# Another program order for the ranking stage of layer 1 in a four-layer graph network

## The chip, the cores and the metric

One core of a Trainium2 chip runs the whole program in one launch. The metric is the device time in microseconds (us); the figure of a kernel is the median of its runs. Five engines work from queues of their own, each in the order of the program: TensorE (PE, with its weight loads shown as PEld), VectorE (DVE), ScalarE (ACT), GpSimd (POOL) and SyncE (SP, which issues most transfers).

## The reference

Four residual layers work on 2708 nodes with 128 features and one dense 2708 x 2708 matrix `adj`. Layer 1, in which the change lies, is a graph attention:

```python
h = jnp.maximum(_layernorm(x), 0.0)
XW = jnp.matmul(h, W)
s_col = jnp.matmul(XW, a[0, :f])
s_row = jnp.matmul(XW, a[0, f:])
Z1 = leaky_relu(s_row[:, None] + s_col[None, :], negative_slope=0.01)
den = jnp.exp(Z1)
num = jnp.matmul(A, den)
att = jnp.where(num != 0, den / jnp.where(num != 0, num, 1.0), 0.0)
x = x + jnp.matmul(A, jnp.matmul(att, XW))
```

`den[i, j]` depends on the two terms `s_row[i]` and `s_col[j]` alone and has a kink where their sum is zero. So the kernel does not multiply `A` by the whole of `den`: it sorts the nodes by `s_row`, takes running sums of the sorted rows of `A` (the "knots"), and for each column picks the two knots around its own kink.

## The kernel before, in words

The nodes lie in T = 22 tiles of 128 (the last has 20), in six groups of four tiles (`GROUPS`, the last has two). The 2708 columns are cut into six pieces of 512 (`KBS`, the last has 148). The stage of the change ranks the nodes by their row term and begins at line 1519 with one loop over the 22 tiles. PE, DVE, ACT and some POOL instructions are pinned (`pe`, `dve`, `act`, `pin`): each engine executes them in the order in which the Python code emits them, so moving a call in the loop moves its instructions in the queue of each engine that it uses.

For each tile t the loop calls:

- `mask(t)` (DVE): a bf16 row of ones where a later node's row term is not above that of the tile's node. Three buffers (`flags`, bufs=3) hold the masks of tiles 1 to 21, so `mask(t)` waits until PE and ACT are done with the mask of tile t - 3. `mask0` has a buffer of its own. Masks get shorter with t, since only columns from the tile on are compared.
- `summed(t)` (ACT): the mask's sum along the row, into `later`; its written copy (`lists`) is a by-product. Tiles 2, 19 and 20 (`SUMMED_HERE`) are summed by DVE while the mask is made.
- `counts(t)` (PE): ones times the mask, added up over the tiles in the two PSUM tiles `cnt`.

Every four tiles a group's counts are complete. `count_row(b)` (ACT) copies them out as a row, `count_turn(b)` (PE) turns that row into a column of `c_ps`, and `ranked(b)` (DVE) takes from it `later` and a constant, which gives the rank of each node. `listed(t0, t1)` (DVE, seven operations) turns ranks into a tile and a place and builds one-hot lists; `joined(t0, t1)` (PE, two matmuls for each tile) adds these lists into the PSUM tile `sp`. When all 22 tiles are joined, `sp` holds for every sorted place the number of its node; DVE copies that into `src_u`, and POOL starts the gathers `mov<-in_adj_dram` with it (`fetch`).

Between these run three others:

- `totals(n)` (PE): the next n block sums. One of them is 16 matmuls over a tile of `adj` with the weights `w_a` (the first eight, FRONT = 8) or `w_n` (the others), into two PSUM tiles `tot`, which shows in the profile as `acc<-chunk,w_a` and the like (`res`, `chunkY`, `chunkU` are other buffers of the same). The argument `TOTALS` says after which tile how many are done: four block sums (0 to 3) run ahead of the loop, 17 in it, one after it. When block sum 7 is done, ACT copies its two halves out with a factor (`act.mul`, output `tots`), and the PSUM tiles are taken anew by block sum 8. SP loads the matrix tiles (line 1233); each load waits for a buffer that an earlier block sum releases.
- `column_terms(g)` (PE): the column terms of group g, eight matmuls for four tiles, into `c_ps`.
- `column_max()` and `node_terms()` (DVE, PE, POOL, ACT): the greatest column term, and factors made of it that are read behind the stage.

`split_terms()` (POOL) is not touched. Where a helper records an operation, the profile names line 84 for it, so groups are told apart by their tiles: `mask`, `lists` (ACT: the mask sums), `row`, `tots`, `rank`, `later`, `tile_of`, `in_tile`, `in_place`, `in_tile_v`, `ps<-mask,ones_b` (counts), `acc<-ident,row` (count turns), `acc<-wga,h1T` (column terms), `acc<-in_tile_v,in_place` and `acc<-lists` (joins).

Of the kernel before, what the change touches and what calls it, by code (L numbers as in the profile page):

```python
# [8 lines left out]
F32 = mybir.dt.float32  # L9
# [8 lines left out]
P = 128  # L18
# [6 lines left out]
def kernel(  # L25
# [21 lines left out]
    T = -(-N // P)  # L47
# [14 lines left out]
    keep = ctx.enter_context(tc.tile_pool(name="keep", bufs=1))  # L62
# [23 lines left out]
    pe, dve, act = Ordered(nc.tensor), Ordered(nc.vector), Ordered(nc.scalar)  # L86
# [683 lines left out]
    FRONT = 8  # L770
# [298 lines left out]
    def column_terms(g):  # L1069
        for t in range(*GROUPS[g]):  # L1070
            pin(
                nc.tensor.matmul(
                    c_ps[0][: width(t), CC + t : CC + t + 1], hT[:, cols(t)], wga[:, 0:1], start=True, stop=True
                )
            )
# [105 lines left out]
    hi, rmax, part = vec("hi", 1), vec("rmax", 1), vec("part", 1)  # L1181
# [19 lines left out]
    tot = [acc(1), acc(2)]  # L1201
    QUARTER = N // 4
    SPLIT = QUARTER // 2
# [33 lines left out]
    so_far, tots = [0], []  # L1237

    def totals(n):
        for x_ in range(so_far[0], so_far[0] + n):  # L1240
            t = todo[x_]
            w = width(t)
            c = early.pop(t, None) or total_chunk(t)
            if x_ == FRONT:
                tot[:] = [acc(1), acc(2)]
            ws_ = w_a if x_ < FRONT else w_n
            for half in range(2):
                for g in range(4):
                    k0 = QUARTER * g + SPLIT * half
                    n_ = (SPLIT, QUARTER - SPLIT)[half]  # L1250
                    pe.matmul(
                        tot[half][32 * g : 32 * g + 32, :n_],
                        ws_[:w, t : t + 1].to_broadcast([w, 32]),
                        c[:w, k0 : k0 + n_],
                        start=(x_ in (0, FRONT)),
                        stop=(x_ in (FRONT - 1, T - 1)),
                    )
            if x_ == FRONT - 1:
                tots.append(keep.tile([P, QUARTER], F32, name="tots", tag="own"))
                for half in range(2):  # L1260
                    x0 = tots[0][:, SPLIT * half : (SPLIT, QUARTER)[half]]
                    act.mul(x0, tot[half][:, : x0.shape[1]], part)
        so_far[0] += n

    totals(1)
    terms_turned(E3 - 1)
# [98 lines left out]
    def summed(t):  # L1365
        w, a = width(t), t * P
        if t not in SUMMED_HERE:
            act.activation(
                seen[:w, a:], masks[t][:w, a:], AF.Copy, accum_out=later[:w, t : t + 1]
            )  # L1370

    def counts(t):
        w, a = width(t), t * P
        mk = masks.pop(t)
        for b, (k0, n) in enumerate(KBS):
            c0, c1 = max(a, k0), k0 + n
            if c0 >= c1:
                continue
            g = 32 * (b % 4)
            pe.matmul(  # L1380
                cnt[b // 4][g : g + 32, c0 - k0 : c1 - k0],
                ones_b[:w, :32],
                mk[:w, c0:c1],
                start=(t == 0),
                stop=(a + w == k0 + n),
            )
# [9 lines left out]
    def count_turn(b):  # L1396
        row = count_rows.pop(b)
        for t in range(*GROUPS[b]):
            o = (t - GROUPS[b][0]) * P
            pe.transpose(  # L1400
                c_ps[0][: width(t), CC + 32 + t : CC + 33 + t], row[:, o : o + width(t)], ident[:1, :1]
            )

    def ranked(b):
        t0, t1 = GROUPS[b]
        for t in range(t0, t1):
            if t in SUMMED_HERE:
                dve.tensor_tensor(
                    later[:, t : t + 1], later[:, t : t + 1], own_later[t], ALU.add
                )  # L1410
        dve.tensor_tensor(
            later[:, t0:t1], later[:, t0:t1], behind[:, t0:t1], ALU.subtract
        )
        for c0, c1, w in ((t0, min(t1, T - 1), P), (max(t0, T - 1), t1, TAIL)):
            if c0 < c1:
                dve.tensor_tensor(
                    rank[:w, c0:c1], c_ps[0][:w, CC + 32 + c0 : CC + 32 + c1], later[:w, c0:c1], ALU.subtract
                )
# [7 lines left out]
    def in_spare(first):  # L1426
        box(
            first,
            8,
            (  # L1430
                spare.tile([P, 8, T], BF16, name="in_tile"),
                spare.tile([P, 8, P + 3], BF16, name="in_place"),
                spare.tile([P, 5, 8, T], BF16, name="in_tile_v"),
            ),
        )
# [11 lines left out]
    def listed(t0, t1):  # L1447

        n = t1 - t0
        (ta, pl, tv), i = boxes[t0]  # L1450
        r_, a_, m_ = rank[:, t0:t1], tile_of[:, t0:t1], at_of[:, t0:t1]
        dve.tensor_scalar(a_, r_, -(PER + 1) / 2.0, 1.0 / PER, op0=ALU.add, op1=ALU.mult)
        dve.tensor_scalar(a_, a_, 1.5 * BIG, None, op0=ALU.add)
        dve.tensor_scalar(a_, a_, -1.5 * BIG, None, op0=ALU.add)
        dve.scalar_tensor_tensor(m_, a_, -float(PER), r_, op0=ALU.mult, op1=ALU.add)
        dve.tensor_tensor(
            ta[:, i : i + n, :],
            at_tile[:, None, :].to_broadcast([P, n, T]),
            a_[:, :, None].to_broadcast([P, n, T]),
            ALU.is_equal,  # L1460
        )
        dve.tensor_tensor(
            pl[:, i : i + n, :],
            at_place[:, None, :].to_broadcast([P, n, P + 3]),
            m_[:, :, None].to_broadcast([P, n, P + 3]),
            ALU.is_equal,
        )
        dve.tensor_tensor(
            tv[:, :, i : i + n, :],
            ta[:, None, i : i + n, :].to_broadcast([P, 5, n, T]),  # L1470
            vals[:, :, t0:t1, None].to_broadcast([P, 5, n, T]),
            ALU.mult,
        )

    def joined(t0, t1):
        for t in range(t0, t1):
            (_, pl, tv), i = boxes.pop(t)
            w = width(t)
            pe.matmul(
                sp[:3, :LIST].rearrange("p (v t) -> p v t", t=T)[:, 2:, 1:],  # L1480
                pl[:w, i, DUP],
                tv[:w, 2:, i, : T - 1],
                start=False,
                stop=False,
            )
            pe.matmul(
                sp[:, :LIST], pl[:w, i, :P], tv[:w, :, i, :], start=False, stop=(t == T - 1)
            )
# [6 lines left out]
    def column_max():  # L1495
        dve.tensor_copy(c_nat[:, : T - 1], c_ps[0][:, CC : CC + T - 1])
        dve.tensor_copy(c_nat[:TAIL, T - 1 :], c_ps[0][:TAIL, CC + T - 1 : CC + T])
        dve.tensor_reduce(c_hi, c_nat, AX.X, ALU.max)
        pe.matmul(
            c_ps[0][:, 256:384], c_hi.to_broadcast([P, P]), ident, start=True, stop=True  # L1500
        )

    def node_terms():
        dve.tensor_reduce(cmax, c_ps[0][:, 256:384], AX.X, ALU.max)
        dve.tensor_scalar(cmx, cmax, rmax, -1.0, op0=ALU.add, op1=ALU.mult)
        pin(nc.gpsimd.tensor_scalar(c_n, c_nat, rmax, None, op0=ALU.add))
        pin(nc.gpsimd.tensor_scalar(hb, c_n, 0.0, -0.495, op0=ALU.max, op1=ALU.mult))
        act.activation(s_n, c_n, AF.Exp, scale=0.99)
        act.activation(sig, hb, AF.Exp)
# [6 lines left out]
        pin(nc.gpsimd.tensor_tensor(parts_of_r[:, 1, :], parts_of_r[:, 0, :], vals[:, 3, :], ALU.subtract))  # L1516
        pin(nc.gpsimd.tensor_copy(vals[:, 4, :], parts_of_r[:, 1, :]))

    TOTALS = {2: 2, 10: 2, **{t: 1 for t in (0, 1, 4, 5, 6, 7, 8, 9, 12, 13, 14, 16, 18)}}
    for t in range(T):  # L1520
        mask(t)
        if t % 4 == 1 and 5 <= t < T - 1:
            ranked(t // 4 - 1)
        if t == 1:
            split_terms()
        if t == 5:
            column_max()
        if t == 6:
            node_terms()
        if t == 10:  # L1530
            in_spare(0)
            listed(0, 8)
        if t == 14:
            in_spare(8)
            listed(8, 12)
        summed(t)
        counts(t)
        if t % 4 == 3:
            count_row(t // 4)
        if t % 4 == 0 and t:  # L1540
            count_turn(t // 4 - 1)
        if t == 11:
            joined(0, 8)
        if t == 15:
            joined(8, 12)
        if t in (1, 2, 3, 4):
            column_terms(t + 1)
        totals(TOTALS.get(t, 0))
    listed(12, 16)
    in_lists(16, T - 16)  # L1550
    ranked(4)
    listed(16, 20)
# [1 line left out]
    count_turn(5)  # L1554
    ranked(5)
    listed(20, T)
    joined(12, T)


    sg = lay.tile([P, N], BF16, name="sg", tag="H")  # L1560
# [89 lines left out]
    for half in range(2):  # L1650
        x0 = tots[0][:, SPLIT * half : (SPLIT, QUARTER)[half]]
# [353 lines left out]
```

## Time and profile before

| | |
|---|---|
| median of 3 runs | 1107.77 us (1105.91 to 1108.09) |
| the profiled execution | 1104.28 us, span 1102.6 us |
| PE busy | 993.3 us (90% of the span), 3553 instructions |
| DVE busy | 582.5 us (53%), 1194 instructions |
| ACT busy | 401.0 us (36%), 629 instructions |
| POOL busy | 228.7 us (21%), 248 instructions |
| DMA | 282.72 MB, mean 256 GB/s |

The busy shares are means over very different stages. The loop over the 22 tiles lies between about 420 and 468 us of the span; the gathers of sorted rows and the writing of knots follow up to about 615 us, the attention up to about 776 us, and layers 2 and 3 fill the rest. The profile names the chain of work that ended last, gives each instruction's start and length by engine, what ended the idle time ahead of it, and the clock that TensorE was granted in any window (1.00 is the full clock). Times of matmuls overlap a little, because they are pipelined and their ends are modelled. All times in the text are from the start of the span.

### The profile page before, as it was taken

To read this page: it belongs to the slowest core of one execution; us is meant where nothing else is said; L and a number is where in the kernel's file an instruction comes from. 1 tells how busy PE (TensorE), PEld (TensorE's weight loads), DVE (VectorE), ACT (ScalarE), POOL (GpSimd) and SP (SyncE) were. 2 spreads that over 40 slices of the span, in tenths; PEclk is the share of its full clock that TensorE was granted. 3 is DMA by queue.
4 is the path that set the end of the run, shared out by engine and by line. 5 is a ranking of instruction groups with operands and counts; after the bars stand their busy time and mean duration, and the time that the engine had idled before them with its cause. 6 is when DMAs were issued, how large, how long until landed. Compare 5 with 4: busy or idle time off the path is not lost.

```text
span 1102.6 us, 10164 instructions
## 1 busy us (share of the span) xinstructions
PE 993.3 (90%) x3553; PEld 485.9 (44%) x3553; DVE 582.5 (53%) x1194; ACT 401.0 (36%) x629; POOL 228.7 (21%) x248
## 2 busy tenths in 40 slices
PE   6999999999999988899787277777999999999998
PEld 5444443444344455554333133333444455455444
DVE  5366368999852266757466489998210321032003
ACT  5100045444300067568765287786200210021000
POOL 2000000000199781023232145551000000000000
PEclk9999999999999998989999769999999999999999
DMA  9997220004389349399999899999999257716811
GB/s 271 342 321 250 66 74 9 0 1 174 132 351 408 113 141 421 131 351 425 420 417 402 292 425 431 428 433 388 398 345 391 88 208 275 264 60 211 303 42 51
DMA packets 48323, 282.72 MB, mean 256 GB/s; under 512 B 6478, under 2 KB 17834, under 8 KB 28660
## 3 DMA queue, kind: packets, MB, share of 16 engines
q1 hardware_dynamic: 38191, 189.13, 45.9%
q0 software_dynamic: 9840, 92.94, 20.9%
q8 instruction: 28, 0.46, 0.2%
q14 instruction: 24, 0.20, 0.0%
q10 hardware_dynamic: 240, 0.00, 0.0%
HBM read 250.06 MB, written 33.00 MB: 257 GB/s over the span
## 4 chain that ended last, share of the span: by engine, by line
PE 66%; DMA 20%; DVE 6%; ACT 3%; issue 3%; POOL 1%; SPq 0%; DVEq 0%; POOLq 0%; ACTq 0%
PE acc L404 34%; PE acc L84 15%; PE acc L806 10%; DMA pair<-table,pair_u 10%; DMA mov<-in_adj_dram,src_u 6%; PE ps L84 3%; DVE att L84 2%; DMA chunk<-in_adj_dram 2%; PE ps L384 1%; ACT att L84 1%; DMA held<-in_adj_dram 1%; PE acc L814 1%; DMA gath<-ydr,near_p 1%; DMA w<-in_L_gnn_W_dram 1%; ACT sg L1567 1%
## 5 line engine op out<-in xcount | busy, mean ns | idle before, releaser
L84 PE MATMUL acc<-att,xw 128*128 128x512 f32 (+2 forms) x264 | 110.6, 570 | 54.3 <-DVE att L84 54.2
L404 PE MATMUL acc<-chunk,h 128*128 128x512 f32 (+1 forms) x384 | 148.0, 542 | 0.0
L84 PE MATMUL acc<-mov,wt 128*128 128x512 f32 (+1 forms) x264 | 109.9, 562 | 19.4 <-DVE mov L84 19.2
L806 PE MATMUL acc<-zT 128*128 128x512 f32 (+2 forms) x264 | 112.3, 559 | 0.0
L404 PEld LDWEIGHTS acc<-chunk,h 128*128 128x128 f32 x384 | 68.8, 190 | 74.1 <-issue 74.1
L84 PEld LDWEIGHTS acc<-att,xw 128*128 128x128 f32 (+1 forms) x264 | 50.0, 197 | 114.8 <-issue 82.6
L942 POOL DMA_INDIRECT gath<-ydr,near_u x63 | 65.1, 1034 | 153.8 <-DMA ydr<-y 140.6
L404 PE MATMUL acc<-chunk,y 128*128 128x512 f32 x204 | 80.2, 553 | 3.9 <-DMA chunk<-in_adj_dram 3.0
L84 PEld LDWEIGHTS acc<-mov,wt 128*128 128x128 f32 x264 | 47.4, 192 | 81.6 <-DVE mov L84 48.0
L821 ACT COPY strip<-acc 128x512 f32<-128x512 f32 (+1 forms) x132 | 60.4, 560 | 59.2 <-issue 35.8
L1790 POOL DMA_INDIRECT pair<-table,pair_u x22 | 64.1, 2913 | 78.6 <-DVE att L84 52.7
L84 DVE SCALAR_TENSOR_TENSOR att<-pair,kap 128x2708 f32<-128x2708 f32 (+3 forms) x24 | 67.1, 2803 | 22.6 <-DMA pair<-table,pair_u 22.6
L84 DVE COPY mov<-knots 2x512 f32<-2x512 f32 x126 | 46.5, 394 | 53.1 <-DMA mov<-in_adj_dram,src_u 32.1
L404 PE MATMUL acc<-chunk,attended 128*128 128x512 f32 x192 | 73.1, 542 | 0.0
L84 ACT ACTIVATE att<-att,sca 128x2708 f32<-128x2708 f32 (+3 forms) x24 | 56.7, 2362 | 41.7 <-DVE att L84 29.0
L84 DVE SCALAR_TENSOR_TENSOR att<-row_all,inv_s,att 128x2708 f32<-128x2708 f32 (+3 forms) x24 | 67.1, 2798 | 3.8 <-ACT att L84 3.8
L823 DVE MAX8 top_v<-strip 128x8 f32<-128x2708 f32 (+1 forms) x22 | 64.7, 2965 | 7.3 <-ACT strip L821 7.3
L806 PEld LDWEIGHTS acc<-zT 128*128 128x128 f32 (+1 forms) x264 | 45.1, 185 | 51.3 <-issue 43.8
L404 PEld LDWEIGHTS acc<-chunk,y 128*128 128x128 f32 x204 | 37.3, 193 | 46.0 <-issue 44.7
L84 ACT ACTIVATE att<-att,hb 128x2708 f32<-128x2708 f32 (+3 forms) x24 | 56.7, 2364 | 0.8
L1567 ACT ACTIVATE sg<-row_all,c_nat 128x2708 bf16<-128x2708 f32 (+1 forms) x22 | 56.4, 2564 | 0.1
L84 ACT COPY knots<-acc 128x512 f32<-128x512 f32 x66 | 37.3, 594 | 42.4 <-PE acc L84 42.2
(379 smaller groups left out, 1277.4 us busy)
## 6 DMA issues: line engine op xcount, KB each, us to landing
chunk<-in_adj_dram SPq DMA_DIRECT2D x75, 1354.0 KB
table<-knots SPq DMA_DIRECT2D x19, 1354.0 KB
res<-in_adj_dram SPq DMA_DIRECT2D x9, 1354.0 KB
held<-in_adj_dram SPq DMA_DIRECT2D x11, 512.0 KB
held<-in_adj_dram SPq DMA_DIRECT2D x16, 256.0 KB
upper<-in_adj_dram SPq DMA_DIRECT2D x4, 842.0 KB
held<-in_adj_dram SPq DMA_DIRECT2D x3, 1024.0 KB
chunkY<-in_adj_dram SPq DMA_DIRECT2D x2, 1354.0 KB
```

Of the source, the lines that this page charges most:

```text
L84: return lambda *a, **k: pin(getattr(self.engine, name)(*a, **k))
L384: mm = nc.tensor.matmul(p[: width(t), t - t0, :], srcT[:, cols(t)], w, start=True, stop=True)
L404: nc.tensor.matmul(out[b][:, :n], y[r, tile_at(i), :], chunk(i)[r, k0 : k0 + n], start=(i == 0), stop=(i == T - 2),)
L806: mm = nc.tensor.matmul(zz[b][:w, :n], zT[:, cols(t)], zT[:, k0 : k0 + n], start=True, stop=False)
L814: nc.tensor.matmul(zz[b][:w, :n], ones_b[g : g + 3, :w], sq_rows[g : g + 3, k0 : k0 + n], start=False, stop=True,)
L821: copied = nc.scalar.copy(s[:w, k0 : k0 + n], zz[b][:w, :n])
L823: nc.vector.max(top_v[:w, t, :], s[:w, :])
L942: nc.gpsimd.indirect_dma_start(out=g[: idx.shape[0], :], out_offset=None, in_=ydr[:, :], in_offset=bass.IndirectOffsetOnAxis(ap=idx, axis=0),)
L1567: nc.scalar.activation(sg[:w, :], row_all[:w, :], AF.Sign, bias=c_nat[:w, t : t + 1], accum_out=signs[:w, t : t + 1],)
L1790: nc.gpsimd.indirect_dma_start(out=r[:w].rearrange("p a n -> p (a n)"), out_offset=None, in_=table[:, :], in_offset=bass.IndirectOffsetOnA ...
```

## The change

It changes only where the calls of this stage stand. The factor copies become a function of their own, `front_total`, called at tile 5 behind the mask sum of that tile instead of right behind block sum 7 (at tile 2). `TOTALS` spreads the same 17 block sums differently. Count turns come at tiles 5, 9, 13, 17 and 20 instead of 4, 8, 12, 16 and 20. The ranks of groups 0 and 1 are taken together at tile 10, those of groups 2 and 3 together at tile 18, instead of one group at each of tiles 5, 9, 13 and 17. The listings are 0 to 7 at tile 10, 8 to 15 at tile 18, then 16 to 19 and 20 to 21 behind the loop; before they were 0 to 7 at tile 10, 8 to 11 at tile 14, and 12 to 15, 16 to 19 and 20 to 21 behind the loop. The joins follow at tiles 12 and 19 and behind the loop. The column terms of groups 2 to 5 move from tiles 1 to 4 to tiles 3 to 6, the column maximum from tile 5 to 12 and the node terms from 6 to 13. The operations are the same, but for the two listings of four tiles that become one of eight, seven DVE instructions for fourteen (DVE has 6 instruction rows fewer, the other engines as many as before).

```diff
--- before.py
+++ after.py
@@ -1255,12 +1255,13 @@
                         start=(x_ in (0, FRONT)),
                         stop=(x_ in (FRONT - 1, T - 1)),
                     )
-            if x_ == FRONT - 1:
-                tots.append(keep.tile([P, QUARTER], F32, name="tots", tag="own"))
-                for half in range(2):
-                    x0 = tots[0][:, SPLIT * half : (SPLIT, QUARTER)[half]]
-                    act.mul(x0, tot[half][:, : x0.shape[1]], part)
         so_far[0] += n
+
+    def front_total():
+        tots.append(keep.tile([P, QUARTER], F32, name="tots", tag="own"))
+        for half in range(2):
+            x0 = tots[0][:, SPLIT * half : (SPLIT, QUARTER)[half]]
+            act.mul(x0, tot[half][:, : x0.shape[1]], part)
 
     totals(1)
     terms_turned(E3 - 1)
@@ -1516,37 +1517,42 @@
         pin(nc.gpsimd.tensor_tensor(parts_of_r[:, 1, :], parts_of_r[:, 0, :], vals[:, 3, :], ALU.subtract))
         pin(nc.gpsimd.tensor_copy(vals[:, 4, :], parts_of_r[:, 1, :]))
 
-    TOTALS = {2: 2, 10: 2, **{t: 1 for t in (0, 1, 4, 5, 6, 7, 8, 9, 12, 13, 14, 16, 18)}}
+    TOTALS = {9: 2, 11: 2, **{t: 1 for t in (0, 1, 2, 3, 7, 8, 10, 12, 13, 14, 15, 16, 17)}}
     for t in range(T):
         mask(t)
-        if t % 4 == 1 and 5 <= t < T - 1:
-            ranked(t // 4 - 1)
         if t == 1:
             split_terms()
-        if t == 5:
-            column_max()
-        if t == 6:
-            node_terms()
         if t == 10:
+            ranked(0)
+            ranked(1)
             in_spare(0)
             listed(0, 8)
-        if t == 14:
+        if t == 12:
+            column_max()
+        if t == 13:
+            node_terms()
+        if t == 18:
+            ranked(2)
+            ranked(3)
             in_spare(8)
-            listed(8, 12)
+            listed(8, 16)
         summed(t)
+        if t == 5:
+            front_total()
         counts(t)
         if t % 4 == 3:
             count_row(t // 4)
-        if t % 4 == 0 and t:
+        if t % 4 == 1 and t > 1 and t < 20:
             count_turn(t // 4 - 1)
-        if t == 11:
+        if t == 12:
             joined(0, 8)
-        if t == 15:
-            joined(8, 12)
-        if t in (1, 2, 3, 4):
-            column_terms(t + 1)
+        if t == 19:
+            joined(8, 16)
+        if t == 20:
+            count_turn(4)
+        if t in (3, 4, 5, 6):
+            column_terms(t - 1)
         totals(TOTALS.get(t, 0))
-    listed(12, 16)
     in_lists(16, T - 16)
     ranked(4)
     listed(16, 20)
@@ -1554,7 +1560,7 @@
     count_turn(5)
     ranked(5)
     listed(20, T)
-    joined(12, T)
+    joined(16, T)
 
 
     sg = lay.tile([P, N], BF16, name="sg", tag="H")
```

## The prediction

> **What bounds the kernel now.** I read the page first: its chain of work is 66% TensorE (PE) and 20% DMA, but that is a mean over stages, so I went to the chain cut to the ranking stage (385 to 480 us), then to the timelines of PE, ACT and DVE there, then to the clock by windows. First the chain (start us, length us, what):
>
> ```profile
> 430.24 2.22 ACT lists L84 x2
> 432.46 0.47 ACT row L84
> 432.97 0.44 PE ps L84 x5
> 434.46 3.14 PE acc L84 x18
> ...
> 461.23 0.61 DVE in_place L84
> 467.29 0.78 PE acc L84 x4
> 469.39 5.09 DMA mov<-in_adj_dram,src_u
> ```
>
> The stage ends when the list of nodes is on PSUM (467.29 + 0.78) and the first gather of rows, `mov`, can start. Up to 459 the chain is mostly PE; after that DVE listings. Where the early loss comes from is in the timelines (start, length, what, in brackets the idle time before it and its releaser), ACT's first and PE's next:
>
> ```profile
> 429.23 1.12 ACT L84 ACTIVATE tots<-acc,part 128x338 f32<-128x338 f32 x2 [3.25 <-PE acc L84]
> 430.24 2.13 ACT L84 ACTIVATE lists<-mask 128x2324 bf16<-128x2324 bf16 x1
> ```
>
> ```profile
> 432.97 0.44 PE L84 MATMUL ps<-mask,ones_b 128*32 128x512 bf16 x5 [2.00 <-ACT row L84]
> 434.39 2.48 PE L84 MATMUL acc<-res,w_n 20*32 20x338 f32 x16
> 440.47 1.34 PE L84 MATMUL acc<-chunkU,w_n 128*32 128x338 f32 x16
> 449.37 2.29 PE L84 MATMUL acc<-in_tile_v,in_place 128*3 128x63 bf16 x16
> 456.35 1.18 PE L84 MATMUL acc<-in_tile_v,in_place 128*3 128x63 bf16 x8
> 465.08 1.48 PE L84 MATMUL acc<-lists 128*3 128x63 bf16 x8 [0.69 <-DVE lists L84]
> ```
>
> ACT, first in its queue, waits 3.25 us with the factor copies (`tots`) for block sum 7; the sum of mask 3 behind it starts late, the count row behind that too, and PE, at count turn 0, stands 2.00 us. Then the same 16 matmuls of a block sum take 2.48 instead of about 1.3 us. The windows show why (length, busy time and count of PE, PEld, DVE, ACT, POOL, then the granted clock, the DMA share and GB/s):
>
> ```profile
> 434.00:436.00 2.00, 2.00 (x16) 0.94 (x20) 1.46 (x6) 1.97 (x3) 1.10 (x1) 0.50 1.02 433
> 440.00:442.00 2.00, 2.00 (x34) 1.17 (x30) 1.84 (x4) 1.34 (x2) 0.00 (x0) 0.90 1.02 433
> 448.00:452.00 4.00, 3.72 (x36) 1.99 (x28) 2.97 (x8) 2.79 (x4) 0.00 (x0) 1.00 0.53 168
> 464.00:468.00 4.00, 2.57 (x15) 1.28 (x14) 2.89 (x13) 0.00 (x0) 0.00 (x0) 0.53 0.00 0
> ```
>
> After the 2.00 us gap the clock is 0.50 from about 434 to 440 us; it is 0.53 again at 464, after PE's small gaps in the tail. Two block sums at 2.48 instead of 1.3 us, and the small work between them, cost some 3 us, and the gap 2.
>
> **The loop, part by part.** Moving an edit helps only if count turn 3 comes earlier, since `ranked` for tiles 8 to 15 (here, as in 12 to 15 before) waits for it. Before, that rank runs at 458.23. For after, I lay the rows of before in the new order.
>
> ACT starts at 420.94 as now. Start to start, its items took: sums of masks 0, 1, 3: 2.59, 2.45, 2.12; row 0.47; sums 4, 5: 2.15, 1.93; factor copies 1.01 (now behind sum 5, when block sum 7 is long done, so its wait is gone); sum 6 1.89; sum 7 1.81. Together 16.42: sum 7 ends at 437.36. That frees the third mask buffer for mask 10 on DVE: 437.40 + 1.07 = 438.47. Now the moved ranks: five small operations at 0.15 to 0.2, 0.8 us; then the listing of tiles 0 to 7 (444.91 to 448.00, 3.09) to 442.36, mask 11 (448.00 to 449.01) to 443.37. PE has little left before that and waits there: I count gaps of about 0.8 (mask 9), 0.8 (row 1) and 1.3 us (mask 11). So the one gap of 2.00 becomes three smaller ones; none reaches 2.00, and a gap of 1.51 us before 413.99 left the clock at 1.00.
>
> From counts 11 at 443.41 PE runs through. The stretch 449.14 to 458.19 of before (9.05 us: counts 11 to 16, 16 join matmuls, turn 2, block sums 16 to 18, 8 join matmuls, turn 3) is the nearest. After has in addition counts 17 (0.2), four more block sums (from 452.25 to 453.42 one takes 1.17: 4.68) and the maximum's matmul (about 0.4), and not the 8 joins (1.06 on the chain): 9.05 + 0.2 + 4.68 + 0.4 - 1.06 = 13.27. Turn 3 ends at 456.68, the rank starts at 456.72: **1.5 us gained**.
>
> **The tail.** Before it takes 458.23 to 468.05 = 9.82 us. After, from the rank: rank, later, rank 0.46; the listing of eight tiles, now behind these ranks and ahead of mask 19, 3.09; mask 19 0.65 (458.84 to 459.49); hop 0.04. Only now PE, which after block sum 20 and counts 18 has been idle some 2.9 us, does counts 19 (0.2), and behind it in its queue the 16 join matmuls (2.29), counts 20 (0.2) and count turn 4 (0.40), for which DVE's rank 4 waits. Sum 7.37 with the hop. Then as before: rank 0.19, listing 16 to 19 2.08, ranks 0.68, last listing 1.55, last join 0.80: 5.30. Total 12.67, **2.85 us longer**. The change takes the listing of tiles 12 to 15 (1.98) out of the end, but puts that of 8 to 11 in with it, and puts the whole join on PE in front of turn 4.
>
> **The clock in the tail.** A gap of 2.9 us on PE is longer than the 2.00 that halved the clock. Eight joins took 1.48 at 465.08 under the half clock and 1.18 at 456.35 under the full one, so 16 take 2.96 instead of 2.29; with counts 20 and turn 4 about 0.85 us more. Bounds: 0 (no drop) and 1.3 (all of these 2.9 us times the 1.48 a row of 2.29 could lose). I take 0.85, by the row of the same operation after the drop.
>
> [...]
>
> **Sum.** -1.5 + 2.85 + 0.85 = +2.2 us on the profiled execution's 1104.28 us (span 1102.6): 1106.5. The median of the runs lies 3.5 us above that execution, so I put the same 2.2 on 1107.77: 1110.0.
>
> **Costed at nothing.** Column terms two tiles later: still 22 small matmuls, about 1 us for eight, in PE time that waits for masks anyway; if that cover were gone they cost what they cost before. Column maximum and node terms: POOL's 1.8 us and ACT's two 0.2 us operations lie near 445, and their reader, `kn`, comes past 468. SP's loads keep their order; each waits for a buffer that a block sum frees. The last one was issued at 448.92 when block sum 15 was done, comes about 1 us later, and is read past 471, with a DMA share of 0.02 at 456 to 460; exposed, it would cost that 1 us. POOL's gathers wait only for the node list. Behind the stage the DMA share is 1.01 from 476 to 580 and 0.98 from 615 to 760, so gathers and table writes carry a later start to the end.
>
> **Rivals.** (1) The tail keeps its clock: +1.35, no measurable difference (this kernel's measurement can tell about 0.2%, 2.2 us, from no change). For it: 1.51 us of gap did nothing. Against: 2.00 did. (2) The three gaps of the loop come so near each other (436 to 443.4) that the clock falls there too: block sums 10 to 14 lose 1.1 each, of which the gap before mask 11 swallows 1.3 and the block sums behind it lose more: +2 to +3, in all +4.2 to +5.2. Also, if other executions of before lack the drop at 434, their 3 us cannot be won. (3) Not slower: PE alone bounds the loop. If the gaps of 2.9 us vanished, because ACT reached the end of sum 6 some 1.7 us sooner than 435.55, turn 3 would end at 453.8 and the sum without clock loss would be 2.85 - 4.4 = -1.5. It decides from a rank before 455.4. For it: the drop in before hides how fast PE would go; against: ACT's row of work has no gap to give. (4) That it does nothing: if the rank waited for less than turn 3 the listing could go earlier; but one operation in it needs tiles 12 to 15.
>
> **How the numbers follow.** Forecast (half clock in the tail, +1.5 to +3.2) 0.45; rival 1 0.22; rival 2 0.17; rival 3 and other gains 0.16. The forecast's 2.2 lies on the bound of 0.2%, and its half above that, rival 2 and a part of the spread of before's runs (1105.91 to 1108.09) make slower by over 0.2% 0.47; within 0.2% 0.39; faster 0.14. Range: from -1.9 (rival 3 with some spread) to +5.2 (rival 2): 1105.9 to 1113.0.
>
> **What would show it.** Right: `tots` without a wait on ACT; no 2.00 us gap on PE at count turn 0 and a clock of 1.00 from 434 to 440; the rank ahead of the long listing at about 456.7; a PE gap of about 2.9 us before a mask matmul near 461; 16 joins directly behind it, taking 2.3 or 3.0 us; the last join ending at 469.4 to 470.3. Wrong: a rank before 455.4, or turn 4 ahead of the joins, or a start of `mov` that is shifted without the end being shifted.

## The result, and the profile after

| | before | after |
|---|---|---|
| median of the runs | 1106.86 us (1103.47 to 1115.85) | 1110.79 us (1107.8 to 1118.67) |
| the profiled execution | 1104.28 us, span 1102.6 | 1110.97 us, span 1109.2 |
| stage: first `mask` on DVE to the end of the last join | 48.27 us | 53.26 us |
| of it, up to the rank of the group that ends the loop | 38.45 us | 39.94 us |
| of it, from there on (the tail) | 9.82 us | 13.32 us |

The ratio of the times is 1.0042, 95% interval [1.0023, 1.006]: slower by 4.65 us (2.5 to 6.6). The time forecast, 1110.0, is near 1110.79, but part of that agreement is luck: before's median was 1106.86 in these runs and not 1107.77, so the change cost about twice the 2.2 us of the sum, and of its two parts the loop came out with the wrong sign.

The two profiled spans differ by 6.6 us. The stage begins 1.49 us earlier in after (418.29 instead of 419.78) and takes 4.99 us longer; the stretch from the first gather of rows `mov` to the first gather `pair` takes 154.18 instead of 151.05 us; the rest to the end is equal (482.13 and 482.16). The 3.1 us of the middle stretch did not repeat: the same changed kernel took 150.54 there in another execution, before 150.11, and the other variants 149.8 to 152.8. The stretch behind it varies as well: it was 486.8 us in E12 and 487.2 in E5. So all comparisons below go by the stage, whose lengths repeat better: 48.27 and 48.33 for before, 53.26 and 52.82 for after.

First the chain of waits of after, cut to the stage (start, length, what):

```profile
431.62 0.54 ACT tots L84
432.16 1.80 ACT lists L84 x2
...
435.82 0.59 ACT row L84
436.44 0.31 PE ps L84
436.76 2.38 PE acc L84 x14
...
458.23 0.16 DVE rank L84
...
460.81 1.07 DVE in_tile_v L84
...
462.71 2.75 PE acc L84 x15
...
470.79 0.78 PE acc L84 x4
...
472.89 5.02 DMA mov<-in_adj_dram,src_u
```

Up to 436 us the chain runs through ACT, where before it had come to PE at 433; the tail shows the listing on DVE, and then the 15 joins on PE that follow it one behind the other. ACT's timeline of after shows what was late at 436:

```profile
431.20 0.96 ACT L84 ACTIVATE tots<-acc,part 128x338 f32<-128x338 f32 x2
432.05 1.81 ACT L84 ACTIVATE lists<-mask 128x1940 bf16<-128x1940 bf16 x1
433.99 1.71 ACT L84 ACTIVATE lists<-mask 128x1812 bf16<-128x1812 bf16 x1
435.82 0.58 ACT L84 COPY row<-ps 1x512 f32<-1x512 f32 x1
```

The factor copies (`tots`) wait for nothing now (3.25 us before). But behind them ACT has the sums of masks 6 and 7 and only then count row 1. PE's timeline of after shows who waits for that row:

```profile
431.78 2.48 PE L84 MATMUL acc<-res,w_n 20*32 20x338 f32 x16 [0.43 <-ACT tots L84]
436.44 0.61 PE L84 MATMUL ps<-mask,ones_b 128*32 128x512 bf16 x4 [2.19 <-ACT row L84]
436.55 2.77 PE L84 MATMUL acc<-chunkY,w_n 128*32 128x338 f32 x16
439.68 0.58 PE L84 MATMUL acc<-ident,row 1*128 1x1 f32 x4
...
445.00 0.38 PE L84 MATMUL ps<-mask,ones_b 128*32 128x512 bf16 x1 [0.24 <-DVE mask L84]
...
462.20 0.57 PE L84 MATMUL ps<-mask,ones_b 128*32 128x128 bf16 x2 [2.64 <-DVE mask L84]
462.49 2.96 PE L84 MATMUL acc<-in_tile_v,in_place 128*3 128x63 bf16 x16
465.62 0.58 PE L84 MATMUL acc<-ident,row 1*128 1x1 f32 x4
468.57 1.48 PE L84 MATMUL acc<-lists 128*3 128x63 bf16 x8 [1.54 <-DVE lists L84]
```

The 2.00 us wait on ACT at counts 4 is gone, and counts 8 stand 2.19 us for the next count row. In PE's queue a block sum (`chunkY`) and counts 9 lie between that and count turn 1 (439.68), which the first ranks wait for. The tail is the one forecast: a wait of 2.64 us for mask 19, then all 16 joins, then turn 4. The clock, by windows (length, busy time and count of PE, PEld, DVE, ACT, POOL, granted clock, DMA share, GB/s):

```profile
431.00:431.50 0.50, 0.35 (x7) 0.04 (x6) 0.17 (x1) 0.50 (x3) 0.00 (x0) 0.95 0.98 412
431.50:432.00 0.50, 0.22 (x4) 0.20 (x8) 0.50 (x2) 0.50 (x2) 0.00 (x0) 0.50 0.92 390
434.00:436.00 2.00, 0.26 (x4) 0.10 (x1) 1.39 (x3) 1.98 (x3) 0.00 (x0) 0.50 1.03 425
441.50:442.00 0.50, 0.50 (x12) 0.14 (x7) 0.50 (x3) 0.00 (x0) 0.00 (x0) 0.81 0.66 282
448.00:452.00 4.00, 4.00 (x40) 2.02 (x39) 2.04 (x6) 3.49 (x10) 0.00 (x0) 1.00 0.00 0
464.00:466.00 2.00, 2.00 (x14) 1.19 (x13) 0.00 (x0) 0.00 (x0) 0.00 (x0) 0.50 0.00 0
```

The clock is at half from 431.45 to about 441.7 (0.95 in one half microsecond puts the fall 0.05 us ahead of its end; 0.81 puts the rise 0.31 us ahead of 442) and again in the tail. The fall in the loop comes before the 2.19 us gap, not behind it.

### The profile page after: what moved, and what is told of

It is laid out like the page before. It is cut to its first block, busy times and chain, and to the rows that moved or that the text cites. A ratio compares the mean times of both kernels' runs of the same rounds, so it can differ in the third digit from the quotient of the medians.

```text
span 1109.2 us, 10157 instructions
## 1 busy us (share of the span) xinstructions
PE 994.6 (90%) x3553; PEld 484.2 (44%) x3553; DVE 582.5 (53%) x1187; ACT 400.5 (36%) x629; POOL 228.8 (21%) x248
## 4 chain that ended last, share of the span: by engine, by line
PE 63%; DMA 22%; DVE 6%; ACT 4%; issue 3%; POOL 1%; SPq 0%; DVEq 0%; POOLq 0%; ACTq 0%
PE acc L404 34%; PE acc L84 13%; PE acc L806 10%; DMA pair<-table,pair_u 10%; DMA mov<-in_adj_dram,src_u 7%; DVE att L84 3%; PE ps L84 2%; DMA chunk<-in_adj_dram 2%; PE ps L384 1%; ACT att L84 1%; DMA held<-in_adj_dram 1%; PE acc L814 1%; DMA gath<-ydr,near_p 1%; ACT lists L84 1%; DMA w<-in_L_gnn_W_dram 1%
## 5 line engine op out<-in xcount | busy, mean ns | idle before, releaser
L84 PE MATMUL acc<-mov,wt 128*128 128x512 f32 (+1 forms) x264 | 112.5, 574 | 20.6 <-DVE mov L84 19.7
```

The lines of the kernel that those rows point to most:

```text
L84: return lambda *a, **k: pin(getattr(self.engine, name)(*a, **k))
```

## The experiments

In the table the loop ends with the rank of tiles 8 to 15 (in the kernels that rank one group at a time, of 12 to 15). Ratios are to before on the same chip; those without one ran once, for the profile. In the profiles of E1 and E7 the stage began under half the clock; a second profile of each, in which it did not or only for 3 us, stands below it.

| kernel | loop | tail | stage | ratio |
|---|---|---|---|---|
| before | 38.45 | 9.82 | 48.27 | 1 |
| before, once more (E10) | 38.50 | 9.83 | 48.33 | |
| after | 39.94 | 13.32 | 53.26 | 1.0042 [1.0023, 1.006] |
| after, once more (E9) | 39.94 | 12.88 | 52.82 | |
| E1, tail as before (half clock at first) | 42.96 | 10.65 | 53.61 | 1.0012 [0.9993, 1.003] |
| E12, the same | 39.55 | 10.64 | 50.19 | |
| E2, front as before | 38.76 | 12.75 | 51.51 | 1.0035 [1.0006, 1.0063] |
| E3, column terms early | 40.65 | 13.32 | 53.97 | 1.0064 [1.0036, 1.0092] |
| E4, masks first, joins last | 40.37 | 9.70 | 50.07 | 1.0025 [1.0004, 1.0047] |
| E7, filler in the front (half clock at first) | 42.84 | 13.30 | 56.14 | 1.0009 [0.9969, 1.0049] |
| E11, the same | 39.57 | 13.32 | 52.89 | |
| E8, filler in the tail | 39.79 | 12.44 | 52.23 | 1.0021 [0.9993, 1.0049] |
| E5, spread | 32.31 | 10.73 | 43.04 | 0.9955 [0.9925, 0.9984] |
| E6, spread further | 31.43 | 10.92 | 42.35 | 0.9936 [0.9912, 0.996] |

All diffs are against the changed kernel.

**E1 and E12: the new front with the tail of before.**

```diff
+        if t in (13, 17):
+            ranked(t // 4 - 1)
-        if t == 18:
-            ranked(2)
-            ranked(3)
+        if t == 14:
-            listed(8, 16)
+            listed(8, 12)
...
+        if t in (12, 16, 20):
...
+        if t == 15:
+            joined(8, 12)
...
+    listed(12, 16)
-    joined(16, T)
+    joined(12, T)
```

> The changed kernel with the tail of the kernel before: count turns 2 and 3 at tiles 12 and 16, ranks at 13 and 17, listings 8 to 11 at tile 14 and 12 to 15 behind the loop, joins at 15 and at the end; everything up to tile 11 as in the changed kernel. Measure: from the start of mask 1 on DVE to the end of the last join on PE, 48.3 us before and 53.3 in the changed kernel; of that 9.8 and 13.3 lie behind the rank of tiles 12 to 15 (the tail), 38.5 and 39.9 ahead of it (the loop). Theory (the tail costs 3.5, the loop 1.5): tail 9.8, whole stage about 49.8, so about 1.5 us slower than before. Rival A (the loss lies behind the stage, where gathers and knots took 3.1 us more): still about 4 us slower than before although the stage is shorter. Rival B (the loop is the loss and the tail only hides it): stage 53, no gain.

The profiled execution of E1 had half the clock in the first 9.5 us of the stage, so its loop (42.96) says nothing of the order. I profiled it again:

> A second profile of the changed kernel with the tail of the kernel before; in the first the clock was at 0.50 during the first 9 us of the stage and again later, and the stage took 53.6 instead of the 49.8 expected. If that was the clock and not the order: tail 9.5 to 10.7, stage 48 to 51 with a full clock at the start. Rival (this order itself has a wait in the loop as long as the tail's saving): 53 again at full clock.

E12 has a tail of 10.64 instead of 13.32, and a loop of 39.55: 1.1 us longer than before's, with a 3.07 us wait at counts 8. So the tail of the change costs 2.7 us against the old tail behind the same front (2.2 by the 12.88 of E9), and the front by itself loses too. The tail is still 0.82 us over that of before. DVE's timeline of E12 has the place:

```profile
459.24 0.16 DVE L84 TENSOR_TENSOR rank<-acc,later 128x4 f32<-128x4 f32 x1 [3.35 <-PE acc L84]
...
461.99 0.23 DVE L84 SCALAR_TENSOR_TENSOR mask<-row_all,r_nat,above 20x20 bf16<-20x20 f32 x1 [0.73 <-PE ps L84]
462.14 0.15 DVE L84 TENSOR_SCALAR tile_of<-rank 128x4 f32<-128x4 f32 x1
```

Mask 21, ahead of the listing, waits 0.73 us for counts, which stand in PE's queue behind the last block sum; the listing begins 2.90 us behind the rank, in before 2.08 (458.23 to 460.31).

**E2: the front of before with the new tail.** Factor copies, column terms, turns 0 and 1, ranks 0 and 1 and the column maximum stand where before had them; what is new is from tile 12 on.

```diff
-    TOTALS = {9: 2, 11: 2, **{t: 1 for t in (0, 1, 2, 3, 7, 8, 10, 12, 13, 14, 15, 16, 17)}}
+    TOTALS = {2: 2, 10: 2, **{t: 1 for t in (0, 1, 4, 5, 6, 7, 8, 9, 13, 14, 15, 16, 17)}}
...
+        if t in (5, 9):
+            ranked(t // 4 - 1)
...
+        if t in (4, 8, 13, 17):
```

> The kernel before up to tile 11 (factor copies at tile 2, column terms at tiles 1 to 4, ranks 0 and 1 at tiles 5 and 9) with the changed tail. Theory: the tail costs 3.5 whatever precedes it, loop about 38.5, stage about 51.8, 3.5 us slower than before. Rival A: near the changed kernel, 4 to 5 slower, with a stage under 52. Rival B: stage about 48.3 to 49, no slower than before.

The loop is 38.76, 0.3 us longer than before's; the tail 12.75, 2.9 us longer. Ratio 1.0035: +3.9 us (0.7 to 7.0). The tail's 2.9 us and the front's 1.1 (E12) to 1.5 (after) make 4.0 to 4.4 of the 4.6 to 5.0 that the whole change costs the stage. Both halves lose.

**E3: column terms back at tiles 1 to 4, the rest as changed.** It asks whether the column terms, moved next to each other, are what holds up the front.

```diff
-        if t in (3, 4, 5, 6):
-            column_terms(t - 1)
+        if t in (1, 2, 3, 4):
+            column_terms(t + 1)
```

> The changed kernel with one thing undone: column terms at tiles 1 to 4, between block sums, instead of 3 to 6, where four groups of them stand with short count matmuls only. Theory (the clock follows what streams through the array, and matmuls of one column stream next to nothing): no fall of the clock at 431 us, where PE was busy by the profile without a gap over 0.45 us; full clock to 436 at least, loop 1 to 2 us shorter than 39.9. Rival (only gaps of PE count): the clock falls at the same place, loop 39.9, time unchanged against the changed kernel. Either way PE still waits at counts 8 for count row 1 on ACT.

The clock fell at 16.9 us of the stage instead of 13.2, but the loop did not get shorter: 40.65. Count row 1 starts 18.24 us into the stage here and 17.53 in after, and counts 8 wait 3.33 us for it. The theory that their place costs the loop its time fell; with them moved back the loop is 0.7 us longer. What is there in after, E1, E12 and E3 alike is a wait of counts 8 for ACT, of 2.19 to 3.33 us.

**E4: masks 19 and 20 ahead of the listing of eight, all its joins at the end.** The same listing, without the queueing behind it.

```diff
-        mask(t)
+        if t not in (19, 20):
+            mask(t)
+        if t == 18:
+            mask(19)
+            mask(20)
...
-        if t == 19:
-            joined(8, 16)
...
-    joined(16, T)
+    joined(8, T)
```

> The changed kernel with masks 19 and 20 made ahead of the listing of tiles 8 to 15, and the 16 joins of those tiles behind the loop, behind count turns 4 and 5. Theory (the tail's price is this queueing: masks behind the listing on DVE, turn 4 behind the joins on PE): from the rank 0.46 + listing 3.09 + mask 21 0.15 + ranks 0.6 + listing 2.0 + ranks 0.68 + listing 1.55 + last joins 0.8 = 9.3 instead of 13.3, the wait for rank 4 (2.97 us) gone, PE's gap of 2.64 us ahead of mask 19's counts gone; stage about 49.3, some 4 us faster than the changed kernel. Rival (the long listing itself is the price): tail 12 or more.

The tail is 9.70 us, that of before (9.82) within 0.2, while the loop, in which the rank now follows the two masks, is 0.43 longer. PE's timeline of E4: turn 4 is done at 463.12, long ahead of the joins, and these run beside DVE's listing of 16 to 19.

```profile
462.72 0.40 PE L84 MATMUL acc<-ident,row 1*128 1x1 f32 x4
464.75 0.17 PE L84 MATMUL ps<-mask,ones_b 20*32 20x20 bf16 x1 [1.63 <-DVE mask L84]
465.39 0.28 PE L84 MATMUL acc<-ident,row 1*128 1x1 f32 x2 [0.47 <-ACT row L84]
465.61 2.90 PE L84 MATMUL acc<-in_tile_v,in_place 128*3 128x63 bf16 x16
```

So it is not the listing of eight tiles that costs the tail its 3.5 us, but what stands behind it in two queues. Of the 3.62 us that the tail gains, 0.43 go to the loop; the stage is 3.2 us shorter than after's. In the whole time (1.0025 against 1.0042) the intervals overlap. The two moves, masks and joins, were made at once, so their shares are not known.

**E8: PE kept busy through the wait of the tail.** Thirteen matmuls of 512 columns, whose result nothing reads, fill the 2.6 us gap ahead of counts 19.

```diff
         counts(t)
+        if t == 18:
+            warm(acc(5), 13)
```

> The changed kernel with 13 extra matmuls of 512 bf16 columns behind counts 18 (about 2.8 us at full clock, result not read), where PE waits 2.64 us for mask 19. Forecast's price of the half clock in the tail (0.85 us): the clock stays at 1.00 to the joins, 16 joins take 2.3 instead of 2.96 us, the tail from the rank of tiles 12 to 15 is about 12.4 to 12.6 instead of 13.3 us. Rival (the clock falls for another reason, or the extra work runs into counts 19): tail 13.3 or longer.

```profile
461.26 2.98 PE L315 MATMUL acc<-ident_b 128*128 128x512 bf16 x13
464.17 0.31 PE L84 MATMUL ps<-mask,ones_b 128*32 128x128 bf16 x2
464.26 2.32 PE L84 MATMUL acc<-in_tile_v,in_place 128*3 128x63 bf16 x16
466.51 0.24 PE L84 MATMUL ps<-mask,ones_b 128*32 128x148 bf16 x1
466.68 0.41 PE L84 MATMUL acc<-ident,row 1*128 1x1 f32 x4
```

The granted clock of E8 is 1.00 from 460 to 466, and PE's timeline has the joins at 2.32 instead of 2.96 us, turn 4 at 0.41 instead of 0.58, and a tail of 12.44 instead of 13.32 and 12.88: without the half clock the tail is 0.4 to 0.9 us shorter. The filler itself holds counts 19 up by 0.2 us (they start 4.17 us behind the rank, in after 3.97), so the half clock costs about 0.6 to 1.1 us. In the whole time (1.0021 against 1.0042) the intervals overlap.

**E7 and E11: PE kept busy in the front.** Four such matmuls behind each of the four groups of column terms.

```diff
+    filler = acc(5)
...
         if t in (3, 4, 5, 6):
             column_terms(t - 1)
+            warm(filler, 4)
```

> The changed kernel with four extra matmuls of 512 bf16 columns (about 0.22 us each at full clock, their result is not read) behind each of the four groups of column terms at tiles 3 to 6: the result of the kernel is unchanged. Theory (the clock follows the streaming): the extra work keeps the clock at 1.00 through the place where it fell in the changed kernel, 13.2 us behind mask 1; PE comes to block sum 8 about 3 us later but then runs at full clock, so the rank at tile 10 comes no later than 22.0 us behind mask 1 (about 20.5 to 22). Rival (only gaps of PE count): the clock falls there as before, or the extra 3.4 us simply delay everything: rank at 23.5 or later.

E7 had half the clock in the first 9.5 us of the stage, and its rank at tile 10 came at 24.91 us instead of by 22.0; its ratio spans 1. So it settled nothing of the loop. Again:

> A second profile of the changed kernel with four extra matmuls behind each group of column terms; in the first the clock was at 0.50 from the start of the stage and rose 9 us behind mask 1, so the place of interest was not met in the same state. If this one starts at full clock and streaming is what counts, the clock stays at 1.00 from 8 to 20 us behind mask 1, and the rank at tile 10 comes at 20.5 to 22.5. If only gaps count, it falls near 13 us, or the extra work is paid in full: rank at 23.5 or later at full clock.

```profile
438.09 1.34 PE L84 MATMUL acc<-res,w_n 20*32 20x338 f32 x16
439.46 0.40 PE L84 MATMUL ps<-mask,ones_b 128*32 128x512 bf16 x4
439.55 1.45 PE L84 MATMUL acc<-chunkY,w_n 128*32 128x338 f32 x16
441.14 0.40 PE L84 MATMUL acc<-ident,row 1*128 1x1 f32 x4
```

In E11 the clock is 1.00 from 3 us of the stage to its tail. The same block sums take 1.34 and 1.45 instead of 2.48 and 2.77 us, and from the start of counts 8 to turn 1 there are 1.68 us instead of 3.24: the half clock costs after 1.56 us at the place where the first ranks wait. The filler itself makes counts 8 late (19.5 us into the stage, 18.15 in after), so that only 0.37 us of it reach the loop.

**E9 and E10: the changed kernel and the kernel before once more,** for how far their profiles repeat.

> A second profile of the changed kernel, to see what of its stage repeats. In three of the ten profiles so far the stage begins with the clock at 0.50 or falls to it within 3 us, behind the wait for the last gather that lies 6 us ahead of it. If the stage's length depends on when the steps of the clock fall (they come 3.4 us or a multiple of it apart), the tail repeats at 12.5 to 13.5 us and the loop comes out between 38 (no fall) and 44 us (half clock at the start as well); the fall after the column terms is there unless the clock is low already. Rival (all is fixed by the order): 39.9 and 13.3 within 0.3.

> A second profile of the kernel before. By the first theory: tail 9.3 to 10.0, loop from 36.5 us (no fall after the gap of 2.00 us) to 42 (half clock at the start too). By the rival: 38.45 and 9.82 within 0.3.

The PE timeline of E9:

```profile
433.13 1.34 PE L84 MATMUL acc<-res,w_n 20*32 20x338 f32 x16 [0.43 <-ACT tots L84]
437.80 0.61 PE L84 MATMUL ps<-mask,ones_b 128*32 128x512 bf16 x4 [3.33 <-ACT row L84]
437.91 2.76 PE L84 MATMUL acc<-chunkY,w_n 128*32 128x338 f32 x16
```

Here the clock fell later (about 434.7), so the 20-row block sum ran at full speed; counts 8 then waited 1.14 us longer, and the loop is 39.94 as in the first profile of after. ACT's row decides when counts 8 start, not PE. E10 repeats before to 0.1 us: 3.25 us at the factor copies, 2.00 at counts 4, 38.50 and 9.83.

**E5 and E6: a version that follows from this.** Block sums are spread between the column terms and put where counts wait for a row; each group is ranked by itself; the rest is kept for the listings; the joins of 8 to 15 go to the end as in E4. The core of E6 (E5 is alike, with `TOTALS = {7: 2, 9: 4, ...}`, turns at 6, 8, 12, 17, 20 and ranks at 8, 10, 15, 18):

```diff
+    TOTALS = {3: 2, 6: 2, 7: 2, 11: 2, **{t: 1 for t in (0, 4, 9, 10, 15, 16, 18, 19, 21)}}
+    TERMS = {2: 0, 3: 2, 4: 4, 5: 4}
+    TURNS = (4, 8, 13, 16, 21)
+    RANKS = (7, 10, 15, 17)
...
+        if t == 11:
+            in_spare(0)
+            listed(0, 8)
...
+    in_spare(8)
+    listed(8, 16)
...
+    joined(8, T)
```

> A new order, made from what the first four runs showed: block sums 4 to 7 after tiles 0, 1, 3, 4 with a group of column terms between each two, factor copies at tile 5, block sums 8 to 10 after tiles 6 and 7, four at tile 9 to cover the first listing, and five kept for tiles 16 to 21; count turns at tiles 6, 8, 12, 17, 20; ranks one group at a time at tiles 8, 10, 15, 18; listing 8 to 15 behind mask 20, its joins behind the last count turn. [...] Rival A (the loss is behind the stage): no faster than before although the stage is shorter. Rival B (DVE and ACT bind and PE's order does not matter): stage 47 or more.

> As the order before it, with other places of the same kind: column terms at tiles 0, 2, 4, 4, column maximum at 6, node terms at 12, count turns at 4, 8, 13, 16, 21, ranks at 7, 10, 15, 17, first listing at 11 with its joins at 12, second listing wholly behind the loop, block sums two at tiles 3, 6, 7 and 11. Theory: stage 41 to 43 us, within 1 us of the other new order, so that it is the spreading and not one place that counts. Rival B: 47 or more.

```profile
433.86 1.34 PE L84 MATMUL acc<-res,w_n 20*32 20x338 f32 x16
435.13 1.35 PE L84 MATMUL acc<-chunkY,w_n 128*32 128x338 f32 x16
...
438.71 0.49 PE L84 MATMUL ps<-mask,ones_b 128*32 128x148 bf16 x4
439.13 0.41 PE L84 MATMUL acc<-ident,row 1*128 1x1 f32 x4
...
450.07 0.41 PE L84 MATMUL acc<-ident,row 1*128 1x1 f32 x4 [0.18 <-ACT row L84]
...
460.68 0.76 PE L84 MATMUL acc<-lists 128*3 128x63 bf16 x4 [0.68 <-DVE lists L84]
```

And E5, PE's timeline around counts 8 (the third row):

```profile
434.02 2.67 PE L84 MATMUL acc<-chunkY,w_n 128*32 128x338 f32 x16
436.28 1.62 PE L84 MATMUL acc<-chunkU,w_n 128*32 128x338 f32 x16
438.24 0.40 PE L84 MATMUL ps<-mask,ones_b 128*32 128x512 bf16 x4
```

E6 has the lowest time of all, 0.9936 [0.9912, 0.996] of before: 7.1 us (4.4 to 9.8) less; E5 has 0.9955, and the intervals of the two overlap. In E5, counts 8 do not wait: two block sums stand just ahead of them. In PE's timeline of E6 no wait of the loop is longer than 0.2 us, and the longest of the tail is 0.68. The stage is 42.35 us, 5.9 less than before's. E5 was laid out to keep the clock up in the loop, and the clock was at half from 433.28 to 436.70 all the same (in E6 from 422.58 to 426.0). Several edits are in each of them at once; how much each is worth was not taken apart.

## Why the prediction was right or wrong

**Right: ACT's row of work.** The copies no longer wait, and the sum of mask 7 ends 17.41 us into the stage (418.29 to 435.70); the rows of before had given 17.58.

**Wrong: what follows count row 1.** The loop was to become 1.5 us shorter and became 1.5 longer. The step that failed is the one that laid the first ranks right behind mask 10, 18.69 us into the stage (438.47 less 419.78); they ran at 22.01. I had put a gap of 0.8 us at row 1, where PE stood 2.19, and nothing between that row and turn 1. The trace has counts 8, a block sum and counts 9 there. Counts 8 wait for the row, since both use the PSUM tiles of the counts; E9, E8, E12 and E3 wait 3.07 to 3.33 us at the same place. With the work behind them at full clock (1.68 us in E11) the ranks would have come 1.76 us later than laid out: 22.01 less 1.56 is 20.45, less 18.69. The half clock adds the other 1.56. Of the sum, 3.32 us, 3.00 arrive at the rank of tiles 8 to 15 (39.94 instead of 36.94), since the first ranks took 0.46 us up to the listing and not the 0.8 laid out.

The error began in the reading of before. I named its row `ps<-mask` with the 2.00 us wait "count turn 0". A count turn is `acc<-ident,row`; that row is counts 4, which wait for count row 0. Read rightly, it says that the counts behind every complete group need ACT's copy of its row. What that costs is the time from PE's coming to them to ACT's being done with the row. The change put the factor copies, with no wait of their own, ahead of row 1; and it left PE with less to do until then: between counts 4 and counts 8 before has four block sums, after has one.

E5 shows that the second part matters. Its copies stand at the same place, and ACT is done with row 1 18.11 us into the stage, as in after. But PE has done two block sums more and comes to counts 8 at 19.42 us, where after's PE came at 15.97 and waited. No run changed the place of the block sums alone.

**Right: PE from counts 11 on.** Forecast 13.27 us to the end of turn 3; it ran from 445.00 to 458.19, 13.19.

**Right: the tail.** 12.67 and 0.85 for the clock make 13.52; measured were 13.32 and 12.88. The wait ahead of mask 19 is 2.64 us (2.9 forecast) and the 16 joins take 2.96 with turn 4 behind them. E4 shows that the queueing is the price, E8 that the clock in it is worth about 0.6 to 1.1. The upper bound of 1.3 us for the clock does not follow from the rows named for it: 1.48 for 1.18 on 2.9 us gives 0.74, less than the 0.85 taken.

**The rivals.** (1) The tail's clock fell (0.50 from 464 to 466), so it is out. (2) The clock did fall in the loop, and the cost of the whole, 4.65 us, lies in this rival's 4.2 to 5.2, but not for its reason: it was to come from three gaps close together and to cost block sums; it came before the gap, and its 1.56 us are half of the loop's miss. So the sign set for the forecast, a clock of 1.00 from 434 to 440, failed: it was 0.50 there. (3) PE did not bound the loop alone; the rank came at 458.23 and not before 455.4. In another order it can come far earlier (31.43 us in E6). (4) The listing and the wait for turn 3 stood where the order puts them.

**Costed at nothing** were the column maximum, node terms and loads, and the time from `pair` on is the same. The column terms are 28 matmul rows in the profile of before and not 22. Whether they were free is open: with the short counts around them they are what ran ahead of the fall of the clock (see the last section).

**Not settled:** whether the clock's fall in the loop would be worth more than 0.37 us without the filler's own time; E11 can't tell, and E3 did not prevent the fall.

## What to carry to other kernels

When an instruction that waited is moved in its queue, ask for every later item of that queue who waits for it, and lay out what stands behind that waiter in its own queue: a wait that vanishes at one place can come back at the next one of the same kind, and all the more when the waiting engine's other work is moved away with it. Read the operands of the waiting row before giving it a name; here that would have shown that the counts behind each group depend on such a row. And before one large step is put where its engine has slack, look at what queues behind it on both engines: the listing of eight cost 3.5 us with masks and joins in the wrong order, and some 0.3 in a better one.

## What the runs showed of the hardware

The clock fell without a gap. In after PE was busy from 424.5 us on, with no gap over 0.45, and fell at 431.45 behind a stretch of mostly column terms and short counts. In E6, which puts two groups of column terms next to each other at 419.97 and 421.48, it fell at 422.58, with no gap from 417 on. In E9 the fall came at 434.67, 0.2 us after the long gap had begun. E11, with 16 matmuls of 512 columns among the same column terms, kept 1.00 there (422.4 us to its tail). E7, with the same filler, kept it too from 429.6 us to its tail (467.2). A reading of mine that fits these is that the clock follows what is streamed and not whether PE is busy by the profile. It is not shown: only the filler runs test it, and they change the timing too. Against it stands E5, where block sums were spread among the column terms and the clock fell at 433.28 in the middle of a block sum (432.30 to 433.88).

The stretches of half clock in the loop were 3.4 us long in E5 and E6, 6.83 in before (433.55 to 440.38) and in E9, and 10.24 in after (431.45 to 441.69), near one, two and three times the shortest. What sets these lengths, and when a stretch begins, was not shown.

Half the clock did not cost all matmuls alike: 16 of a block sum took 2.47 (E1) instead of 1.35 us, eight column terms 1.87 (E1) instead of 1.05, 16 joins 2.96 (after) instead of 2.32 (E8).
